# Pairs of PSUM banks for the counts of a graph layer: one copy for two node groups

## The chip, the cores and the metric

The kernel runs on one core of one Trainium2 chip. The metric is the device time of one execution in microseconds, the median over several runs; lower is better. One execution was also profiled, and its trace is what the readings below come from.

## The reference

One layer of a graph network over 12,500 nodes with 128 features and 200,000 edges, of 4 types, sorted by target node:

```python
h = jnp.maximum(_layernorm(x, axis=-1), 0.0)
xs = h[src]
for i in range(4):                        # edge types
    mask = (edge_type_4 == i)[:, None]
    msgs = msgs + jnp.where(mask, xs @ W[i] + b[i], 0.0)
x = x + jax.ops.segment_sum(msgs, dst, num_segments=12500)
```

The targets are drawn as 12500 * u**2, so low node numbers get very many edges and high ones few.

## The kernel before

The kernel works in three stretches: a preparation (up to about 200 us), a long middle (to about 1550 us), and a short end.

**Preparation.** Every row of x is normalized and put as a table `htab` of three 16-bit parts in device memory. The first 568 chunks of 128 edges (the "dense" edges, with low target nodes) are sorted into slots.

**The middle** weaves two kinds of work into one stream of instructions, whose order for TensorE (PE), VectorE (DVE) and ScalarE (ACT) is the order in which the code emits them. SyncE (SP) and GpSimd (POOL) get theirs from a scheduler.

*The dense work* (`dense_work`) takes the dense target nodes in 19 batches of up to 31 units; a unit is a group of up to three nodes or node groups (580 units in all). For each batch:

- `count` makes, for each unit, a matrix of how often each source node (and edge type) occurs. DVE makes two one-hot matrices per slot (`o2`, L1068, and `o1`, L1076), three sets of slots ahead. One matmul per slot (L1101) adds to a count bank of 396 columns; a unit has one or two slots, now and then more. The finished bank is copied to the SBUF tile `counts` by ACT (L1109). The copy is not emitted at once: it goes into the list `owed`, and the function `settle(owed)` emits it when the next unit is finished, or when another user of the same pool asks for a bank.
- `multiply` passes over the table for a batch that is already counted: SP loads three table rows of 128 nodes at a time (`hs`, five buffers), ACT decodes the counts into `dec` (L1169, four buffers, emitted two loads ahead), and PE adds up into the bank `pa` (L1215 with the raw counts, L1207 with `dec`). At the end ACT copies `pa` to `sd` (L1253), and `tail` multiplies it by the weights (L1260); DVE adds the result to `acc` (L1279).

While a batch is counted, the one before it is multiplied. `dense_work` takes whichever of the two is less far along, with the count kept ahead, so that steps of one matmul of the count alternate with steps of six matmuls of the pass.

*The sparse work* takes the other chunks of 128 edges in groups of up to 16. POOL gathers the rows of `htab` (L590), DVE makes one-hots (L608), and in `sum_up` PE multiplies four chunks into one bank `ps` (L643), so that a full group fills four of them, which ACT copies to `sb` (L633). This copy waits in a list of its own, `sums_owed`, until the next `ps` bank is asked for. Between the third and the fourth `ps` bank, `weigh` takes a bank for the group's own counts (four short matmuls, L660), which ACT copies to `cnt` (L664) at once; later it forms `py` (L667, L669), which DVE adds to a ring of sums (L732). From time to time a piece of the ring is transposed (`leave`, L765), added to x by DVE (L770) and stored. Seven times `prep_steps` transposes indices of edges (L375, L376), which ACT copies out.

**The PSUM banks** of a core are eight, and before the change they are given out so: the pool `x_ps` has four single banks, for the count of a unit, for `tail`, `leave`, `prep_steps` and the group counts of `weigh`; `s_ps` has two, for `ps`; `y_ps` and `a_ps` have one each, for `py` and `pa`. A pool gives a new tile any of its banks that is free, and the first writer waits for the last reader of what lay there.

**The end** begins when the dense work is done (`dense_out` is set): the last sparse groups, and the transposes and stores of all dense nodes.

Of the kernel before, what the change touches and what calls it, by code (L numbers as in the profile page):

```python
# [35 lines left out]
F32 = mybir.dt.float32  # L36
# [10 lines left out]
PSUM = bass.MemoryType.PSUM  # L47
# [3 lines left out]
P = 128  # L51
EPS = 1e-5
UN = 3
G = 16
SG = 4
WIN = 32
ROOM = 6
C0 = 568
UB = 31
# [10 lines left out]
OT = 4  # L70
# [17 lines left out]
def kernel(  # L88
# [10 lines left out]
    nc = tc.nc  # L99
    N, D = x.shape  # L100
    E = src.shape[0]
    NT, _, DO = w.shape
# [18 lines left out]
    q = E0 / E  # L121
# [92 lines left out]
    NB = NW * NT  # L214
# [62 lines left out]
    spool = mid.enter_context(tc.tile_pool(name="typed", bufs=2))  # L277
    x_ps = mid.enter_context(tc.tile_pool(name="x_ps", bufs=4, space=PSUM))
    s_ps = mid.enter_context(tc.tile_pool(name="s_ps", bufs=2, space=PSUM))
    y_ps = mid.enter_context(tc.tile_pool(name="y_ps", bufs=1, space=PSUM))  # L280
    a_ps = mid.enter_context(tc.tile_pool(name="a_ps", bufs=1, space=PSUM))
    raw_room = ExitStack()
    aheads = raw_room.enter_context(tc.tile_pool(name="aheads", bufs=4))
# [63 lines left out]
    def prep_steps(m, prep):  # L347
# [267 lines left out]
    def settle(of):  # L615
        while of:
            of.pop(0)()

    adds = []
    finish = []  # L620
# [28 lines left out]
    def weigh(t0, g, oh, sb, last):  # L649
        win = window_of(C0 + t0)  # L650

        def bank(own):
            settle(owed)
            to = y_ps.tile([P, G * WIN], F32, name="py") if own else x_ps.tile([P, G * WIN], F32, name="pt")
            return to[:, : G * win].rearrange("p (g n) -> p g n", g=G)

        ohv = oh.rearrange("p g (t n) -> p g t n", t=NT)
        pc = bank(False)
        for t in range(NT):
            nc.tensor.matmul(  # L660
                pc[t * CG : (t + 1) * CG, :g, :], three, ohv[:, :g, t, :], start=True, stop=True, tile_position=(0, t * CG)
            )
        cnt = spool.tile([P, G * KM // NT], BF16, name="cnt", bufs=1)[:, : G * win].rearrange("p (g n) -> p g n", g=G)
        nc.scalar.copy(cnt[:, :g], pc[:, :g])  # L664
        yield True
        py = bank(not last)
# [89 lines left out]
    def leave(j0, j1, of, c0):  # L756

        nf = min(j1, N // P) - j0
        xt = seen_out.pop(j0) if j0 in seen_out else fetch(j0, j1)
        settle(owed)  # L760
        pt = x_ps.tile([P, OT, DO], F32, name="pt")
        for j in range(j0, j1):
# [12 lines left out]

        return rest

# [69 lines left out]
    def check_all():  # L847
# [4 lines left out]
        nc.vector.tensor_copy(many[:, 2:3], held)  # L852
        pb = x_ps.tile([P, 3], F32, name="pt")
        ones = outp.tile([P, P], F32, name="ones", bufs=1)
# [189 lines left out]
    def count(now, room):  # L1044
# [6 lines left out]
        order = sorted((n / len(of), i) for of in like.values() for n, i in enumerate(of))  # L1051
        for _, i in order:
# [38 lines left out]
        yield 0.0  # L1091
        counts = now[1] = room().tile([P, NW + 1, UB * NT], I32, name="counts")
        for n, of in enumerate(sets):
            supply(n)
            for k, (i, s, by, first, last) in enumerate(of):
# [3 lines left out]
                if first:  # L1099
                    pb = x_ps.tile([P, NB + NT], F32, name="pt")  # L1100
                one = nc.tensor.matmul(pb, o1, o2, start=first, stop=last)  # L1101
# [4 lines left out]
                if last:  # L1106
                    settle(owed)
                    owed.append(
                        lambda i=i, pb=pb: nc.scalar.copy(  # L1109
                            counts[:, :, i * NT : (i + 1) * NT], pb.rearrange("p (b t) -> p b t", t=NT)  # L1110
                        )
                    )
                done += 1
# [37 lines left out]
    def multiply(now):  # L1151
# [104 lines left out]
        def tail(sd):  # L1256
            settle(owed)
            py = x_ps.tile([P, 3 * UB], F32, name="pt")
            for t in range(NT):
# [21 lines left out]

            tails.append(rest)

# [277 lines left out]
    for gi, (t0, g) in list(enumerate(zip(starts, sizes)))[RAW:]:  # L1561
# [56 lines left out]
        if work is None and not dense_out:  # L1618
# [178 lines left out]
```

## Time and profile before

| | |
|---|---|
| median of 3 runs | 1589.8 us (1585.2 to 1591.06) |
| the profiled execution | 1605.82 us, its span 1604.1 us |
| granted TensorE clock, mean | 0.930 |
| PE busy | 1317.4 us (82%) |
| ACT busy | 1077.8 us (67%) |
| DVE busy | 1004.4 us (63%) |
| POOL busy | 966.3 us (60%) |

A group of instructions is named by its line, its engine, its operation and its tiles (written tile <- read tiles). "Idle before" is time in which the engine stood still ahead of such an instruction, with what ended it; "issue" is time in which nothing that the profile shows was waited for. A row of the timeline gives a start in us from the span's start, a duration in us, and merges instructions of one line that follow each other (x6).

### The profile page before, as it was taken

Reading aid. Unit: us, or ns where it says so; the run is one execution under the profiler, and the core shown is the slowest. Engines: PE = TensorE matmul, PEld = TensorE weight load, DVE = VectorE, ACT = ScalarE, POOL = GpSimd, SP = SyncE. Lnnn points to the kernel's source line nnn. Section 1 sums busy time; section 2 is a strip of 40 time slices with the busy share of each in tenths; the row PEclk is TensorE's granted clock in tenths of the full one; section 3 lists DMA queues with packets and bytes.
Section 4 is the critical chain, followed back from the end, with each engine's and each line's share of the span. In section 5 each row is a group of like instructions: output and inputs, shape, how many; then the busy total and the mean of one; then the engine's idle time right before and its main releaser. Section 6 shows DMA issues by size and latency. Waiting matters only on the chain.

```text
span 1604.1 us, 30332 instructions
## 1 busy us (share of the span) xinstructions
PE 1317.4 (82%) x9232; PEld 899.3 (56%) x9232; DVE 1004.4 (63%) x5138; ACT 1077.8 (67%) x1815; POOL 966.3 (60%) x1024
## 2 busy tenths in 40 slices
PE   4876876688889887988889888888888888888885
PEld 1334654466566665656556565665656565565654
DVE  7784466647677765766665575656656565666524
ACT  5675433577677776777677776877777777767651
POOL 6525566666666666666666665666666666666662
PEclk9885798799999999999999999999999999999997
DMA  7542398476676666667676765766666666656762
GB/s 210 186 168 69 113 294 279 123 240 216 192 219 211 216 200 204 209 206 225 190 228 207 227 212 183 229 200 213 216 215 201 207 207 202 215 187 209 254 190 74
DMA packets 184629, 322.55 MB, mean 201 GB/s; under 512 B 30243, under 2 KB 82524, under 8 KB 184460
## 3 DMA queue, kind: packets, MB, share of 16 engines
q1 hardware_dynamic: 132716, 214.63, 42.1%
q0 software_dynamic: 46992, 96.30, 20.0%
q10 hardware_dynamic: 4752, 9.64, 1.6%
q8 instruction: 73, 1.20, 0.3%
q14 instruction: 96, 0.79, 0.1%
HBM read 294.78 MB, written 25.67 MB: 200 GB/s over the span
## 4 chain that ended last, share of the span: by engine, by line
PE 64%; issue 10%; DMA 8%; ACT 7%; DVE 6%; another core or an unknown queue 4%; SPq 1%; DVEq 0%; ACTq 0%
PE pa L1207 16%; PE pa L1215 15%; PE pt L1101 10%; DMA hs<-dtab 7%; PE py L669 6%; PE ps L643 6%; ACT dec L1169 3%; PE pt L1260 2%; PE pa L1237 1%; ACT counts L1109 1%; DVE o L1068 1%; PE ps L701 1%; DVE o L1076 1%; DVE ring L732 1%
## 5 line engine op out<-in xcount | busy, mean ns | idle before, releaser
L590 POOL DMA_INDIRECT hm<-htab,srcT x947 | 915.0, 966 | 570.0 <-issue 207.0
L1169 ACT ACTIVATE dec<-counts 128x1116 fp32r<-128x1116 uint8 (+1 forms) x594 | 662.2, 1136 | 46.4 <-PE pa L1207 12.6
L1068 DVE TENSOR_SCALAR o<-iota_n,hkT 128x392 bf16<-128x392 f16 x1069 | 354.3, 331 | 387.1 <-PE pt L1101 184.6
L1215 PE MATMUL pa<-counts,hs 128*128 128x372 fp8e4 x1764 | 370.9, 336 | 80.6 <-DMA hs<-dtab 37.1
L1207 PE MATMUL pa<-dec,hs 128*128 128x372 f32 x1764 | 411.9, 364 | 29.6 <-ACT dec L1169 14.9
L1109 ACT CAST counts<-pt 128x396 int32<-128x396 f32 x580 | 278.8, 496 | 184.4 <-PE pt L1101 43.7
L1207 PEld LDWEIGHTS pa<-dec,hs 128*128 128x128 f32 x1764 | 309.0, 193 | 68.7 <-issue 30.1
L1101 PE MATMUL pt<-o,o 128*128 128x396 bf16 x1069 | 292.8, 344 | 53.7 <-issue 27.0
L1215 PEld LDWEIGHTS <-hs 128*128 128x128 f16 x1764 | 160.2, 99 | 234.4 <-issue 81.3
L1076 DVE TENSOR_SCALAR o<-iota_b,loT,byT 128x128 bf16<-128x128 bf16 x647 | 213.4, 330 | 0.0
L643 PE MATMUL ps<-oh,hm 128*128 128x72 bf16 (+7 forms) x2841 | 185.0, 201 | 26.6 <-issue 20.6
L643 PEld LDWEIGHTS <-hm 128*128 128x128 f16 x2841 | 149.4, 101 | 101.9 <-issue 54.4
L732 DVE TENSOR_TENSOR ring<-ring,py 128x18 f32 (+6 forms) x912 | 158.6, 174 | 58.4 <-issue 19.3
L608 DVE TENSOR_SCALAR oh<-iota_b,keyT 128x72 bf16<-128x72 bf16 (+7 forms) x947 | 161.8, 257 | 39.3 <-PE pa L1207 23.4
L633 ACT ACTIVATE sb<-ps 128x288 f32<-128x288 f32 (+8 forms) x237 | 99.5, 421 | 108.0 <-PE ps L643 32.2
L1101 PEld LDWEIGHTS <-o 128*128 128x128 bf16 x1069 | 86.6, 99 | 84.6 <-issue 31.2
L669 PE MATMUL py<-sb,wsb 128*128 128x288 f32 (+6 forms) x456 | 123.6, 414 | 0.8 <-issue 0.8
L1076 DVE TENSOR_SCALAR o<-iota_b,loT 128x128 bf16<-128x128 bf16 x422 | 121.7, 288 | 0.0
L669 PEld LDWEIGHTS py<-sb,wsb 128*128 128x128 f32 x456 | 84.1, 195 | 25.0 <-issue 3.9
L664 ACT CAST cnt<-pt 128x288 bf16<-128x288 f32 (+10 forms) x62 | 24.3, 393 | 96.8 <-remote 38.7
L574 POOL DMA_INDIRECT hx<-in_x_dram,srcT x48 | 46.1, 961 | 39.9 <-DVE varr L493 11.0
L1237 PE MATMUL pa<-counts,hs 128*128 128x264 fp8e4 x294 | 45.8, 300 | 11.9 <-DMA hs<-htab 7.1
(251 smaller groups left out, 804.1 us busy)
## 6 DMA issues: line engine op xcount, KB each, us to landing
hs<-dtab SPq DMA_DIRECT2D x576, 288.0 KB
hm<-htab,srcT POOLq DMA_INDIRECT x947
htab<-h SPq DMA_DIRECT2D x32, 288.0 KB
hs<-htab SPq DMA_DIRECT2D x32, 288.0 KB
dtab<-dec ACTq DMA_DIRECT2D x32, 288.0 KB
xo<-in_x_dram SPq DMA_DIRECT2D x23, 256.0 KB
out_dram<-xo SPq DMA_DIRECT2D x23, 256.0 KB
hm<-in_x_dram SPq DMA_DIRECT2D x18, 192.0 KB
```

The costliest lines, as they stand in the source:

```text
L590: one = nc.gpsimd.indirect_dma_start(out=hm[:, (i - h0) * D3 : (i - h0 + 1) * D3], out_offset=None, in_=htab, in_offset=bass.IndirectOffse ...
L608: nc.vector.tensor_scalar(oh[:, i, :], iota_b[:, :K], keyf[:, at : at + 1], None, ALU.is_equal)
L643: nc.tensor.matmul(ps[:, i - i0, :], rows(i, c), oh[:, i, :], start=(c == 0), stop=(c == 2))
L669: nc.tensor.matmul(py[:, :g, :], wsb[:, t, :], sb[0][:, :g, t, :], start=False, stop=(t == NT - 1))
L732: nc.vector.tensor_tensor(to, to, of(i), ALU.add)
L1068: one = nc.vector.tensor_scalar(o2[:, k, :NB], iota_n, hkT[:, s : s + 1], None, ALU.is_equal)
L1076: one = nc.vector.tensor_scalar(o1[:, k], iota_b, loT[:, s : s + 1], by, ALU.is_equal, ALU.mult)
L1101: one = nc.tensor.matmul(pb, o1, o2, start=first, stop=last)
L1109: lambda i=i, pb=pb: nc.scalar.copy(counts[:, :, i * NT : (i + 1) * NT], pb.rearrange("p (b t) -> p b t", t=NT))
L1169: nc.scalar.activation(decoded[n][:, : j1 - j0, :nv].rearrange("p j (m v) -> p j m v", m=3), by_digit[:, j0:j1, : nu * NT * 4].rearrange(" ...
L1207: nc.tensor.matmul(to.rearrange("p (m v) -> p m v", m=3), row.bitcast(F32R)[:, D // 2 :], decoded[j // DS][:, j % DS, :nv].rearrange("p (m ...
L1215: nc.tensor.matmul(to.rearrange("p (m v) -> p m v", m=3), row[:, :D], counts[:, j, : nu * NT * 4].rearrange("p (v m) -> p m v", m=4)[:, :3 ...
```

## The change

Inside the middle, the four single banks of `x_ps` become two pairs of banks (pool `z_ps`, opened when the preparation ends and closed when the dense work is done).

- Two units that follow each other in `count` write the two banks of one pair, and one ACT instruction copies both (`keep_pair`, 2 x 396 elements in a partition instead of 396). The copy goes into `owed` when the second unit is finished. A batch of 31 units has 15 pairs and a last unit alone.
- `tail`, `leave` and `prep_steps` take a whole pair (`pair()`) and use one bank of it.
- The group counts of `weigh` take a bank of `s_ps`, the pool of two that `ps` uses. Asking for it emits the copy that waits in `sums_owed`, and no longer the one in `owed`.
- Asking for a pair emits what waits in `owed`, and also what waits in a new list `unadded`: DVE's additions out of a pair that `tail` or `leave` filled.
- After the dense work, four single banks are opened again (`x2_ps`), and all runs as before.

```diff
+    unadded = []
+
+    def pair():
+        settle(owed)
+        settle(unadded)
+        return z_ps.tile([P, 2, 512], F32, name="pz")
+
+    def bank():
+        if dense_out:
+            return x_ps.tile([P, 512], F32, name="pt")
+        settle(sums_owed)
+        return s_ps.tile([P, 512], F32, name="ps")
...
-        settle(owed)
-        pg = x_ps.tile([P, 2, P], F32, name="pt")
+        pg = (bank() if dense_out else pair()[:, 0, :])[:, : 2 * P].rearrange("p (q e) -> p q e", q=2)
...
     def weigh(t0, g, oh, sb, last):
...
-        def bank(own):
-            settle(owed)
-            to = y_ps.tile([P, G * WIN], F32, name="py") if own else x_ps.tile([P, G * WIN], F32, name="pt")
+        def bank_of(own):
+            to = y_ps.tile([P, G * WIN], F32, name="py") if own else bank()
...
     def leave(j0, j1, of, c0):
...
-        settle(owed)
-        pt = x_ps.tile([P, OT, DO], F32, name="pt")
+        pt = (bank() if dense_out else pair()[:, 0, :]).rearrange("p (j o) -> p j o", o=DO)
...
-        return rest
+        if dense_out:
+            return rest
+        todo = [rest]
+        unadded.append(lambda: settle(todo))
+        return lambda: settle(todo)
...
+        def keep_pair(pz, us):
+            to = counts.rearrange("p b (i t) -> p i b t", t=NT)
+            to = to[:, us[0] : us[-1] + 1 : max(1, us[-1] - us[0])]
+            nc.scalar.copy(to, pz[:, : len(us), : NB + NT].rearrange("p m (b t) -> p m b t", t=NT))
...
                 if first:
-                    pb = x_ps.tile([P, NB + NT], F32, name="pt")
+                    m = place[i]
+                    if m % 2 == 0:
+                        two = [pair(), sorted(order[m : m + 2])]
+                    pb = two[0][:, two[1].index(i), : NB + NT]
...
                 if last:
                     settle(owed)
-                    owed.append(
-                        lambda i=i, pb=pb: nc.scalar.copy(
-                            counts[:, :, i * NT : (i + 1) * NT], pb.rearrange("p (b t) -> p b t", t=NT)
-                        )
-                    )
+                    if m % 2 or m + 1 == len(order):
+                        owed.append(lambda two=two: keep_pair(*two))
...
         def tail(sd):
-            settle(owed)
-            py = x_ps.tile([P, 3 * UB], F32, name="pt")
+            py = pair()[:, 0, : 3 * UB]
...
-            tails.append(rest)
+            unadded.append(rest)
+            tails.append(lambda: settle(unadded))
...
     building.close()
+    ahead_ps.close()
+    z_ps = ahead_ps.enter_context(tc.tile_pool(name="z_ps", bufs=2, space=PSUM))
...
             counting.close()
+            ahead_ps.close()
+            x_ps = ahead_ps.enter_context(tc.tile_pool(name="x2_ps", bufs=4, space=PSUM))
```

How this moves instructions at the place between the third and the fourth `ps` bank of a group is shown by ACT's order there. The group is the same in both pieces; `ps_9603` and `ps_9396` are its third `ps` bank, `pt_9709` and `ps_9499` the bank of its group counts. ACT before:

```order
L1109 CAST counts_9311<-pt_9565 128x99x4 [waits PE_49]
L1109 CAST counts_9311<-pt_9586 128x99x4 [waits PE_49]
L1169 ACTIVATE dec_9629<-counts_8191 128x1116 [waits Activation_49]
L1169 ACTIVATE dec_9694<-counts_8191 128x1116 [waits PE_49,Activation_49]
L1109 CAST counts_9311<-pt_9626 128x99x4
L1109 CAST counts_9311<-pt_9685 128x99x4 [waits PE_49]
L664 CAST cnt_9714<-pt_9709 128x256 [waits PE_49]
L633 ACTIVATE sb_9519<-ps_9603 128x256
```

ACT with the change:

```order
L1192 ACTIVATE dec_9419<-counts_8023 128x1116 [waits Activation_49]
L1114 CAST counts_9113<-pz_9381 128x2x99x4 [waits PE_49]
L1192 ACTIVATE dec_9485<-counts_8023 128x1116 [waits PE_49,Activation_49]
L646 ACTIVATE sb_9314<-ps_9396 128x256 [waits PE_49]
L676 CAST cnt_9504<-ps_9499 128x256 [waits PE_49]
```

The copy of the third `ps` bank now stands ahead of the copy of the group counts, and there are fewer copies of counts around it.

PE at the same place before; `ps_9721` is the group's fourth `ps` bank:

```order
L660 LDWEIGHTS three_218
L660 MATMUL pt_9709<-oh_9071,three_218 32x256
L660 LDWEIGHTS three_218
L660 MATMUL pt_9709<-oh_9071,three_218 32x256
L643 LDWEIGHTS hm_9018 [waits DMASW4_49]
L643 MATMUL ps_9721<-oh_9071,hm_9018 128x64
L643 LDWEIGHTS hm_9018
```

PE with the change, where `ps_9510` is that fourth bank:

```order
L672 LDWEIGHTS three_218
L672 MATMUL ps_9499<-oh_8877,three_218 32x256
L672 LDWEIGHTS three_218
L672 MATMUL ps_9499<-oh_8877,three_218 32x256
L656 LDWEIGHTS hm_8826 [waits DMASW4_49]
L656 MATMUL ps_9510<-oh_8877,hm_8826 128x64 [waits Activation_49]
L656 LDWEIGHTS hm_8826
```

PE's instructions stand in the same order, but the first matmul into the fourth bank now waits for ACT: its bank is that of `ps_9396`.

A second place, on PE, is where a piece of the ring has just been transposed while a unit was being counted. PE before (`pt_16328`, `pt_16383` and `pt_16389` are the banks of three units that follow each other):

```order
L1101 LDWEIGHTS o1_16184
L1101 MATMUL pt_16328<-o2_1715,o1_16184 128x396
L1207 MATMUL pa_15844<-dec_16257,hs_16330 128x372 x3
L1207 MATMUL pa_15844<-dec_16275,hs_16332 128x372 [waits Activation_49]
L1207 MATMUL pa_15844<-dec_16275,hs_16332 128x372 x2
L1101 LDWEIGHTS o1_16184
L1101 MATMUL pt_16383<-o2_1715,o1_16184 128x396 [waits Activation_49]
L1101 LDWEIGHTS o1_16265 [waits DVE_49]
L1101 MATMUL pt_16389<-o2_1715,o1_16265 128x396 [waits Activation_49]
```

PE with the change (the transposes took the pair `pz_15950`; `pz_15933` is the pair of counts that was open meanwhile, `pz_15994` the next one):

```order
L1127 LDWEIGHTS o1_15792
L1127 MATMUL pz_15933<-o2_1719,o1_15792 128x396
L1230 MATMUL pa_15462<-dec_15863,hs_15935 128x372 x3
L1230 MATMUL pa_15462<-dec_15880,hs_15937 128x372 x3
L1127 LDWEIGHTS o1_15792
L1127 MATMUL pz_15933<-o2_1719,o1_15792 128x396
L1127 LDWEIGHTS o1_15871 [waits DVE_49]
L1127 MATMUL pz_15994<-o2_1719,o1_15871 128x396 [waits Activation_49]
```

The last matmul of one pair is followed at once by the first of the next in both. With the change that one waits for ACT's copy of the very pair just finished, since the transposes hold the other pair; before, it waited for a bank that had been filled earlier, one of four.

More of the change, by code (lines that the diff above doesn't have):

```diff
@@ L281 @@
     a_ps = mid.enter_context(tc.tile_pool(name="a_ps", bufs=1, space=PSUM))
+    ahead_ps = mid.enter_context(ExitStack())
+    x_ps = ahead_ps.enter_context(tc.tile_pool(name="x_ps", bufs=4, space=PSUM))
     raw_room = ExitStack()
@@ L650, in weigh @@
         win = window_of(C0 + t0)
-        def bank(own):
-            settle(owed)
-            to = y_ps.tile([P, G * WIN], F32, name="py") if own else x_ps.tile([P, G * WIN], F32, name="pt")
+        def bank_of(own):
+            to = y_ps.tile([P, G * WIN], F32, name="py") if own else bank()
             return to[:, : G * win].rearrange("p (g n) -> p g n", g=G)
         ohv = oh.rearrange("p g (t n) -> p g t n", t=NT)
-        pc = bank(False)
+        pc = bank_of(False)
         for t in range(NT):
@@ L665, in weigh @@
         yield True
-        py = bank(not last)
+        py = bank_of(not last)
         nc.tensor.matmul(py[:, :g, :], b128, cnt[:, :g, :], start=True, stop=False)
@@ L852, in check_all @@
         nc.vector.tensor_copy(many[:, 2:3], held)
-        pb = x_ps.tile([P, 3], F32, name="pt")
+        pb = bank()[:, :3]
         ones = outp.tile([P, P], F32, name="ones", bufs=1)
@@ L1051, in count @@
         order = sorted((n / len(of), i) for of in like.values() for n, i in enumerate(of))
-        for _, i in order:
+        order = [i for _, i in order]
+        place = {i: m for m, i in enumerate(order)}
+        for i in order:
             of = slots_of(vs[i])
```

1 line of the change is left out of this document (removed).

## The prediction

> **What bounds the kernel now.** I read the page's busy times and its chain first, then the middle as one stretch (the columns are PE, PEld, DVE, ACT, POOL, granted clock, DMA share, GB/s), then what PE waits for.
>
> ```profile
> PE 1317.4 (82%) x9232; PEld 899.3 (56%) x9232; DVE 1004.4 (63%) x5138; ACT 1077.8 (67%) x1815; POOL 966.3 (60%) x1024
> PE 64%; issue 10%; DMA 8%; ACT 7%; DVE 6%; another core or an unknown queue 4%; SPq 1%; DVEq 0%; ACTq 0%
> 300.00:1548.00 1248.00, 1079.75 (x7797) 749.25 (x7794) 781.85 (x4034) 912.08 (x1383) 778.59 (x810) 0.97 0.68 211
> PE pa L1215 <- DMA hs<-dtab: 37.1, 39, 2.4
> PE pa L1207 <- ACT dec L1169: 14.9, 20, 2.6
> PE pa L1215 <- ACT sd L1253: 7.7, 4, 3.5
> PE pt L1101 <- ACT counts L1109: 6.4, 4, 4.1
> PE ps L643 <- ACT sb L633: 4.9, 3, 4.3
> PE pt L1260 <- ACT sd L1253: 4.5, 1, 4.5
> ```
>
> PE makes the chain: 64% of the end time lies on it, and in the middle it is busy 1079.75 of 1248 us (87%), ACT 73%. PE is not full, though: it stands still for 168 us there. Little of that is ACT's doing. The five rows in which work of the middle waits for ACT sum to 14.9 + 7.7 + 6.4 + 4.9 + 4.5 = 38.4 us. So a faster ACT can give 38.4 us at the very most, and PE waits for PSUM banks (the rows of `counts` and `sb`) for only 11.3 us. With four single banks and two for `ps`, banks are hardly ever late. That is what the change puts at risk.
>
> **ACT's saving.**
>
> ```profile
> L1109 ACT CAST counts<-pt 128x396 int32<-128x396 f32 x580 | 278.8, 496 | 184.4 <-PE pt L1101 43.7 <-PE ps L643 38.3 <-remote 32.2
> L1536 ACT COPY xo<-pa 128x512 f32<-128x512 f32 x1 | 0.6, 592 | 0.0
> 176.21 2.87 ACT L1109 CAST counts<-pt 128x396 int32<-128x396 f32 x7
> ```
>
> A copy out of PSUM costs 496 ns for 396 elements and 592 for 512, so 96 / 116 = 0.83 ns an element. A pair (792) then costs 496 + 396 x 0.83 = 824 ns, 168 less than two. Eighteen batches of 31 units and one of 22 make 18 x 15 + 11 = 281 pairs: 281 x 0.168 = 47 us less ACT time. But copies that follow each other overlap: seven took 2.87 us, 410 ns each, 86 less than the row's mean. Between busy neighbours a removed instruction so saves 168 - 86 = 82 ns, in all 23 us. I take 23, since ACT is busy for three quarters of the middle. The Trainium skill ("ScalarE: Activation LUTs", section "What ACT_TABLE_LOAD costs") says that back-to-back ACTIVATEs overlap by about 93 ns; by it the saving would be 75 ns a pair, 21 us, an estimate from that page. The row of seven bears it out, and it speaks against the change: merging instructions saves less than their fixed cost.
>
> 23 us is 2.5% of ACT's 912 us. Of the 38.4 us that PE waits for ACT I take 5 away (nothing below, all 38.4 above).
>
> **Two pairs instead of four banks.** I put the trace's times beside the new order of instructions and asked, at each of the 299 places where a pair of counts is used again, how long after its last matmul the next user's first matmul stands. The median is 4.6 us; for the four single banks the same reading gives 6.3. A pair needs two hand-overs and the copy. A hand-over takes 0.05 us:
>
> ```profile
> 783.88 0.47 ACT L1253 ACTIVATE sd<-pa 128x372 f32<-128x372 f32 x1
> 784.40 1.96 PE L1215 MATMUL pa<-counts,hs 128*128 128x372 fp8e4 x6 [1.07 <-ACT sd L1253]
> 788.48 0.31 PE L660 MATMUL pt<-oh,three 128*32 128x288 bf16 x4
> 788.84 0.40 ACT L664 CAST cnt<-pt 128x288 bf16<-128x288 f32 x1 [1.29 <-PE pt L660]
> ```
>
> ACT ends at 784.35 and PE starts at 784.40; PE ends at 788.79 and ACT starts at 788.84. So a pair is back after 0.05 + 0.82 + 0.05 = 0.92 us if ACT is free. At 29 places there is less time than that, at nine of them none: one shown in the orders above, where transposes hold the other pair. It is this one:
>
> ```profile
> 1092.48 1.16 ACT L1169 ACTIVATE dec<-counts 128x1116 fp32r<-128x1116 uint8 x1
> 1092.60 0.51 PE L1101 MATMUL pt<-o,o 128*128 128x396 bf16 x2
> 1092.94 0.66 PE L1215 MATMUL pa<-counts,hs 128*128 128x372 fp8e4 x3
> ```
>
> The first matmul of the row of two ends one pair (at about 1092.93), the second (from 1092.78) opens the next in the same banks. If ACT were free, PE would stand until 1092.93 + 0.92 = 1093.85, 1.1 us. But ACT decodes until 1093.64, and the copy comes behind that: 1093.64 + 0.82 + 0.05 = 1094.51, 1.7 us. Done so for all 299 places, the sum is 14 us at 29 places with ACT free, and 113 us at 99 places with ACT as late as in the trace (the end of the instruction ahead of the copy in ACT's new order). The first of the 99 is late by 0.2 us at the end of the preparation, the last by 0.8 us near the end of the middle:
>
> ```profile
> 175.48 1.17 PE L1101 MATMUL pt<-o,o 128*128 128x396 bf16 x3
> 176.21 2.87 ACT L1109 CAST counts<-pt 128x396 int32<-128x396 f32 x7
> ...
> 1478.05 1.14 ACT L1169 ACTIVATE dec<-counts 128x1116 fp32r<-128x1116 uint8 x1
> 1479.09 0.50 PE L1101 MATMUL pt<-o,o 128*128 128x396 bf16 x2
> ```
>
> I take 45, between 14 and 113, nearer the lower end: ACT's lateness in the trace holds copies that go, and an ACT for which PE has waited is no longer behind at the next place.
>
> **Group counts in `s_ps`.** Here `ps` loses its slack: the fourth `ps` bank of a group now reuses the third, with only the group counts between. Before, a median of 9 us lay between the uses of a bank. In 38 groups the two stand within 3.5 us of each other, and the evict of the third (0.42 us, L633) must fit in.
>
> ```profile
> L633 ACT ACTIVATE sb<-ps 128x288 f32<-128x288 f32 (+8 forms) x237 | 99.5, 421 | 108.0 <-PE ps L643 32.2
> 313.60 0.32 PE L643 MATMUL ps<-oh,hm 128*128 128x48 bf16 x6
> 315.37 1.14 ACT L1169 ACTIVATE dec<-counts 128x1116 fp32r<-128x1116 uint8 x1
> ...
> 660.04 2.16 ACT L1169 ACTIVATE dec<-counts 128x1116 fp32r<-128x1116 uint8 x2
> 661.25 0.35 PE L643 MATMUL ps<-oh,hm 128*128 128x64 bf16 x6
> ...
> 1352.92 1.16 ACT L1169 ACTIVATE dec<-counts 128x1116 fp32r<-128x1116 uint8 x1
> 1355.49 0.41 PE L643 MATMUL ps<-oh,hm 128*128 128x88 bf16 x6
> ...
> 1524.33 0.43 PE L643 MATMUL ps<-oh,hm 128*128 128x96 bf16 x6
> 1525.47 1.14 ACT L1169 ACTIVATE dec<-counts 128x1116 fp32r<-128x1116 uint8 x1 [1.77 <-PE ps L643]
> ```
>
> These are four of the 38, the first and the last among them: PE's first matmul into the fourth bank, and the work that stands ahead of the evict in ACT's new order. In the group of the orders above that is a pair of decodes which ends at 662.20; with 0.42 for the evict and 0.05 the bank is free at 662.67, 1.4 us after PE wants it at 661.25. Near 1355 the evict is in time: the decode ahead of it ends at 1354.08. Over the 38 groups the sum is 77 us, at 32 of them; with an ACT that is never behind it is nothing. I take 35, for the reason just given.
>
> **What stands behind these waits, and what hides them.** PE takes its queue in order, so behind a wait for a bank stand the matmuls of the pass, of the next counts and of the sparse group; DVE's one-hots (L1068) and POOL's gathers (L590), which wait for PE's progress, come later with it. Some of it is paid back: while PE stands, loads of `hs` and decodes under way go on, and PE finds less of its 37.1 + 14.9 = 52 us of waits for them. I take 35 of these 52 off (bounds 0 and 52).
>
> **Edits at nothing.** `tail`, `leave` and the index transposes take a pair each; that is in the 299 places, since they stand in the rotation. Their DVE additions now come at the next request for a pair, so that a late load of x would hold DVE and the one-hots behind it. Such a wait shows once before (5.2 us, for L770), and DVE is at 63% in the middle: 0, with 20 as an upper end. Opening the pairs waits for the last bank of the preparation, once, about 1 us; PE is idle around it.
>
> **Sum.** -5 + 45 + 35 - 35 = +40 us. The profiled execution has a span of 1604.1 us, which becomes 1644; its own time of 1605.8 becomes 1645.8. It stands 16 us above the median of 1589.8, so the forecast for the median is 1589.8 + 40 = 1630 us.
>
> **The rivals.**
>
> *ACT is in time (faster).* With fewer copies in its queue ACT may no longer be behind when a bank is wanted. Then the pairs cost their 14 us, the `ps` banks nothing, and the 38.4 us of waits for ACT mostly go: 14 - 30 = -16, 1574 us. For it: ACT idles 184.4 us before L1109 and 108.0 before L633, so it is not short of time. Against it: that idle time is waiting for PE, in order, after which ACT runs behind in a burst of copies and decodes, as at 313.60. It decides if ACT's lag at the fourth `ps` bank falls from some 2 us (77 / 38) below about 0.9 us, the least distance of 1.35 us less evict and hand-over. Chance 0.22.
>
> *All cancels (same).* The bank waits are only taken out of PE's other waits: within 8 us of 1590. Within 0.5%, or 8 us, a measurement of this kernel cannot be told from no change. Chance 0.10.
>
> *Full price (much slower).* ACT stays as late as in the trace and nothing is hidden: 113 + 77 - 5 = +185 at the most, with 35 hidden +150, 1740 us. Against it: it takes the lateness of before for granted in a kernel where PE keeps stopping for ACT. Chance 0.13; from 1670 to 1740, with some 0.04 of it under 1695.
>
> *DVE is held by loads of x.* Up to 20 us on top, 1650. One row for it. Chance 0.05.
>
> **The numbers.** The forecast has 0.50, with a range of its own of 1600 to 1670 (the bank waits at half of the 80 that I took, 40 - 5 - 25, and at one and a half times, 120 - 5 - 35). Slower by over 0.5%: 0.50 + 0.13 + 0.05 = 0.68; within: 0.10; faster: 0.22. The range that should hold 8 in 10 runs from 1572 (half of the faster case, 0.11) over the same, the forecast and DVE (0.65) to 1695 (0.04 of the full price).
>
> **What would show it.** Right: PE's waits for the copy of pairs and for `sb` at L656 (the new line of the `ps` matmuls) rise from 11.3 us together to some 60 to 90; ACT's copies are about 299 at 0.82 us, its busy time down by 20 to 50 us; PE's waits for `hs` fall. Wrong: those waits stay under 20 us, or a pair's copy takes clearly more than 0.82 us, or DVE turns up as what PE waits for.

## The result, and the profile after

The changed kernel takes 1611.74 us (median; 1607.01 to 1619.29) where the kernel before takes 1589.8 on the same chip: a ratio of 1.0144 with a 95% interval of 1.0109 to 1.0179, so 22 us slower. The profiled execution took 1619.29 us with a span of 1617.5 us, 13.4 us over the span of before. (The two differences differ because the profiled execution of before stood 16 us above its median, and this one 7.6.)

The page's busy times and its chain by engine, and the same middle stretch as one window (PE, PEld, DVE, ACT, POOL, granted clock, DMA share, GB/s):

```profile
PE 1306.4 (81%) x9232; PEld 918.5 (57%) x9232; DVE 1006.0 (62%) x5138; ACT 1060.3 (66%) x1534; POOL 969.4 (60%) x1024
PE 63%; ACT 13%; issue 8%; DMA 6%; DVE 5%; another core or an unknown queue 4%; POOL 2%; SPq 0%; DVEq 0%; ACTq 0%; POOLq 0%
300.00:1548.00 1248.00, 1055.22 (x7676) 753.67 (x7674) 774.18 (x3990) 884.26 (x1122) 766.42 (x796) 0.96 0.68 208
```

ACT has less to do (1060.3 us against 1077.8), yet its share of the chain has risen from 7% to 13%. In the same 1248 us of the middle PE does 24.5 us less. PE's waits say for what it stands. `pz` is the new name of the pairs; L1127 are the matmuls of the counts, L1282 those of `tail`, L656 those of `ps`, L1238 and L1230 those of the pass:

```profile
PE ps L656 <- ACT sb L646: 53.8, 22, 5.4
PE pz L1127 <- ACT counts L1114: 48.8, 37, 6.5
PE pa L1238 <- DMA hs<-dtab: 19.1, 16, 3.3
PE pz L1127 <- issue: 15.3, 21, 2.2
PE pz L1282 <- ACT counts L1114: 13.1, 7, 5.1
PE pa L1238 <- issue: 7.3, 13, 1.0
PE pa L1230 <- ACT dec L1192: 6.6, 12, 1.0
PE pa L1230 <- issue: 3.3, 5, 1.0
```

Two smaller rows belong beside them:

```profile
PE ps L656 <- DMA hm<-htab,srcT: 11.7, 6, 2.7
PE ps L656 <- ACT dec L1192: 8.6, 6, 3.0
```

The waits for banks were 6.4 + 4.9 = 11.3 us; now the three largest are 53.8 + 48.8 + 13.1 = 115.7 us. But the time in which PE is not busy rose only from 1604.1 - 1317.4 = 286.7 to 1617.5 - 1306.4 = 311.1, by 24.4 us. (The span rose by only 13.4 us because PE's busy time fell by 11.0 us with the same instructions; why it fell is open, and the ends of matmuls are modelled.) So on balance some 80 of the 104 us of new waits were taken out of others. `hs` fell from 37.1 to 19.1. The row of `dec` at L1230 fell from 14.9 to 6.6, but the wait only moved: with L656 and L1238, all rows that end in `dec` came to 19.0 us, against 16.7 before. Waits for `hm` even rose, from 0.9 to 11.7. The largest part came from rows that end in "issue", which before were

```profile
PE pa L1215 <- issue: 32.7, 48, 2.5
PE pt L1101 <- issue: 27.0, 33, 6.3
PE pa L1207 <- issue: 14.3, 29, 1.2
```

so 74.0 us, of which 25.9 are left (all rows that end in "issue": 130.1 and 73.5). Waits for DVE's one-hots fell from 12.8 to 1.8 us and those for `sd` from 12.2 to 2.6. What such idle time consists of the profile does not say; it gives way when PE stands elsewhere.

ACT's groups (line, busy time, mean ns, idle time before), and the copies of counts by themselves (min, median and max in ns, first and last start in us):

```profile
L1114 ACT CAST counts<-pz 128x792 int32<-128x792 f32 (+1 forms) x299 | 238.1, 799 | 155.0 <-PE pz L1127 54.7 <-remote 22.1 <-PE ps L656 20.4
L646 ACT ACTIVATE sb<-ps 128x288 f32<-128x288 f32 (+8 forms) x237 | 97.6, 412 | 186.3 <-PE py L681 80.1 <-remote 37.6 <-PE ps L656 17.9
```

```profile
L1114 ACT CAST counts<-pz x299: 477/818/865, 132.4 to 1506.3; 128x792 int32<-128x792 f32 x132, 128x396 int32<-128x396 f32 x18
```

The copies are 299 as forecast, with a mean of 799 ns. The eighteen single copies are in that mean; the median, nearly always a pair, is 818 ns (forecast 824). By the fixed cost and the rate that the Trainium skill gives for an ACTIVATE with immediate scale and bias ("ScalarE: Activation LUTs", section "What ACT_TABLE_LOAD costs") a pair would take 186 + 792 x 0.833 = 846 ns, an estimate from that page; the trace agrees within 28 ns.

When the loss comes is read from `sd`, which ACT writes once a batch, after and then before, in the same view:

```profile
L1276 ACT ACTIVATE sd<-pa x19: 392/478/483, 281.9 to 1570.4; 128x372 f32<-128x372 f32 x18, 128x264 f32<-128x264 f32 x1
```

```profile
L1253 ACT ACTIVATE sd<-pa x19: 392/480/494, 295.0 to 1555.0; 128x372 f32<-128x372 f32 x18, 128x264 f32<-128x264 f32 x1
```

The first batch ends 13.1 us earlier than before, the last 15.4 us later. So the change gains up to the first batch and loses 28.5 us in the 18 batches that follow.

### The profile page after: what moved, and what is told of

It is laid out like the page before. It is cut to its first block, busy times and chain, and to the rows that moved or that the text cites. A ratio compares the mean times of both kernels' runs of the same rounds, so it can differ in the third digit from the quotient of the medians.

```text
span 1617.5 us, 30046 instructions
## 1 busy us (share of the span) xinstructions
PE 1306.4 (81%) x9232; PEld 918.5 (57%) x9232; DVE 1006.0 (62%) x5138; ACT 1060.3 (66%) x1534; POOL 969.4 (60%) x1024
## 4 chain that ended last, share of the span: by engine, by line
PE 63%; ACT 13%; issue 8%; DMA 6%; DVE 5%; another core or an unknown queue 4%; POOL 2%; SPq 0%; DVEq 0%; ACTq 0%; POOLq 0%
PE pa L1230 17%; PE pa L1238 14%; PE pz L1127 10%; PE py L681 6%; PE ps L656 6%; ACT dec L1192 6%; ACT counts L1114 4%; DMA hs<-dtab 2%; DMA hm<-htab,srcT 2%; POOL hm L590 2%; PE pz L1282 1%; PE pa L1260 1%; DMA hs<-htab 1%; ACT sb L646 1%
## 5 line engine op out<-in xcount | busy, mean ns | idle before, releaser
L1192 ACT ACTIVATE dec<-counts 128x1116 fp32r<-128x1116 uint8 (+1 forms) x594 | 652.1, 1129 | 49.1 <-PE pa L1230 17.7
L1230 PE MATMUL pa<-dec,hs 128*128 128x372 f32 x1764 | 416.6, 370 | 10.6 <-ACT dec L1192 6.6
L1238 PE MATMUL pa<-counts,hs 128*128 128x372 fp8e4 x1764 | 360.0, 336 | 33.4 <-DMA hs<-dtab 19.1
L1127 PE MATMUL pz<-o,o 128*128 128x396 bf16 x1069 | 299.5, 349 | 73.3 <-ACT counts L1114 48.8
L1230 PEld LDWEIGHTS pa<-dec,hs 128*128 128x128 f32 x1764 | 319.4, 199 | 45.9 <-issue 17.3
L1114 ACT CAST counts<-pz 128x792 int32<-128x792 f32 (+1 forms) x299 | 238.1, 799 | 155.0 <-PE pz L1127 54.7
L1238 PEld LDWEIGHTS <-hs 128*128 128x128 f16 x1764 | 166.0, 99 | 196.4 <-issue 69.7
L656 PE MATMUL ps<-oh,hm 128*128 128x72 bf16 (+7 forms) x2841 | 181.7, 202 | 97.9 <-ACT sb L646 53.8
L656 PEld LDWEIGHTS <-hm 128*128 128x128 f16 x2841 | 153.0, 101 | 166.6 <-issue 118.2
L1127 PEld LDWEIGHTS <-o 128*128 128x128 bf16 x1069 | 87.4, 101 | 76.2 <-issue 39.6
L676 ACT CAST cnt<-ps 128x288 bf16<-128x288 f32 (+7 forms) x58 | 23.0, 396 | 71.9 <-PE pz L1127 33.0
```

The source lines that it names most:

```text
L656: nc.tensor.matmul(ps[:, i - i0, :], rows(i, c), oh[:, i, :], start=(c == 0), stop=(c == 2))
L1114: nc.scalar.copy(to, pz[:, : len(us), : NB + NT].rearrange("p m (b t) -> p m b t", t=NT))
L1192: nc.scalar.activation(decoded[n][:, : j1 - j0, :nv].rearrange("p j (m v) -> p j m v", m=3), by_digit[:, j0:j1, : nu * NT * 4].rearrange(" ...
L1230: nc.tensor.matmul(to.rearrange("p (m v) -> p m v", m=3), row.bitcast(F32R)[:, D // 2 :], decoded[j // DS][:, j % DS, :nv].rearrange("p (m ...
L1238: nc.tensor.matmul(to.rearrange("p (m v) -> p m v", m=3), row[:, :D], counts[:, j, : nu * NT * 4].rearrange("p (v m) -> p m v", m=4)[:, :3 ...
```

## The experiments

They ran on three chips, on which the kernel before took 1605.57 us (`a_share` to `c_two`), 1346.12 us (`after_again` to `e_copy`) and 1348.19 us (`f_again` to `b_soon`). Times are therefore compared as ratios to the kernel before on the same chip, and directly only within one of these sets. (A ratio differs by up to 0.2% from the quotient of the two medians given here.) The kernel before has a trace from the first chip alone. My theory: the loss is banks that ACT gives back late. Its rival: the pairs alone, or the group counts in `s_ps` alone, make the loss. A second question came up on the way: whether it matters where a copy stands in ACT's queue. ACT takes this queue in order: in the trace of before, the eight instructions shown above as ACT's order ran in just that order, from 657.42 to 666.65 us.

**One half alone (`a_share`).** The kernel before, with only the group counts moved to `s_ps`.

```diff
-            settle(owed)
-            to = y_ps.tile(...) if own else x_ps.tile([P, G * WIN], F32, name="pt")
+            if own: ...
+            else:
+                settle(sums_owed)
+                to = s_ps.tile([P, 512], F32, name="ps")
```

> The kernel before with one part of the change alone: the group counts of the sparse work lie in the pool of the two ps banks; the four single banks stay for the counts of units. Theory 'banks' (PE's waits for banks make the loss, and both parts have a share of it): about half of the loss, some +10 us over before (1600 us); PE waits for the evicts of ps (sb) for 40 to 55 us, and for copies of counts for under 10 us. Rival 'pairs only' (the pairs make all of the loss, the ps waits are paid back by other waits): within 4 us of before.

Measured: 1608.21 us, ratio 1.0025 (1.0005 to 1.0046). PE's waits:

```profile
PE ps L643 <- ACT sb L633: 63.1, 26, 5.0
PE pa L1222 <- DMA hs<-dtab: 17.3, 19, 2.9
```

The wait for `sb` is as large as in the changed kernel and larger than the 35 us that I took, but it costs only 2.6 us of time (4.0 by the ratio). "Banks" had expected some 10 us, "pairs only" 4 at most. In a kernel with four count banks, PE gets the wait back nearly whole.

**The other half alone (`b_single`, `b_pairs`).** Both leave out the group counts: the four matmuls of `weigh`, their copy to `cnt` and the matmul with the bias (the bias is missing from the sums). `b_single` is otherwise the kernel before, `b_pairs` the changed one, so that between them stand the pairs alone.

```diff
-        pc = bank(False)
-        for t in range(NT):
-            nc.tensor.matmul(pc[t * CG : (t + 1) * CG, :g, :], three, ohv[:, :g, t, :], ...)
-        nc.scalar.copy(cnt[:, :g], pc[:, :g])
...
-        nc.tensor.matmul(py[:, :g, :], b128, cnt[:, :g, :], start=True, stop=False)
```

> The kernel before without the group counts of the sparse work: their four matmuls, their copy and the matmul with the bias are left out of every group, so the output lacks the bias of those edges. It is the base for the next run. Both theories: some 10 to 25 us under before (1565 to 1580), with PE's waits for copies of counts under 10 us.

> The changed kernel without the group counts (the same part left out), so that the pairs of banks act alone and nothing shares the ps banks. Theory 'banks': +8 to +14 us over the run with single banks and no group counts; PE waits for copies of counts for 45 to 65 us, for sb under 10 us. Rival 'ps only' (the shared ps banks make all of the loss): within 4 us of that run, or below it by what ACT saves.

Measured: 1601.36 us, ratio 0.9963 (0.9943 to 0.9983), and 1629.69 us, ratio 1.015 (1.0128 to 1.0173). The pairs alone cost 28.3 us, where "banks" had expected 8 to 14. `b_single` is only 4.2 us under before, where 10 to 25 were expected. PE's waits, of `b_single` first:

```profile
PE pa L1206 <- DMA hs<-dtab: 85.8, 68, 3.3
PE pt L1092 <- ACT counts L1100: 7.3, 9, 2.1
```

```profile
PE pa L1229 <- DMA hs<-dtab: 54.3, 55, 3.8
PE pz L1118 <- ACT counts L1105: 53.1, 40, 5.5
PE pz L1273 <- ACT counts L1105: 15.6, 5, 8.2
PE pz L767 <- ACT counts L1105: 11.3, 6, 3.3
```

On this chip the loss is the pairs', not the shared `s_ps`. Two of the rows are not counts waiting for counts: L1273 is `tail` and L767 is `leave`, 26.9 us in 11 waits. They are few, and each is long: 8.2 us at most.

`b_single` also shows how much slack PE has with four single banks. Its PE has 24.0 us less to do than that of `a_share` (1292.5 us busy against 1316.5) and hardly waits for `sb` (5.6 us at L643), yet its time is only 6.9 us shorter: PE waits 85.8 us for `hs` instead of 17.3. That fits a wait for `sb` standing largely in place of one for `hs`, though no run changes that alone. Why the waits for pairs are not paid in the same way is open.

**Is it the merged instruction (`c_two`)?** The changed kernel, with each bank of a pair copied by an instruction of its own, both at the pair's place.

```diff
-            nc.scalar.copy(to, pz[:, : len(us), : NB + NT].rearrange(...))
+            for k, i in enumerate(us):
+                nc.scalar.copy(counts[:, :, i * NT : (i + 1) * NT], pz[:, k, : NB + NT].rearrange(...))
```

> The changed kernel with each pair copied by two instructions of one bank each, so that ACT's saving is taken back and the banks stay as they are. Theory 'banks': ACT is busy for 20 to 45 us more, the pair comes back 0.1 us later, and the time is 2 to 10 us above the changed kernel (1614 to 1622). Rival 'long copy' (an instruction of 0.82 us that waits for two units holds up the decodes behind it): as fast as the changed kernel or faster, 1600 to 1612.

Measured: 1635.91 us, ratio 1.0205 (1.0183 to 1.0227), more than the 1.0144 of the change. ACT's copies and PE's wait for them:

```profile
L1113 ACT CAST counts<-pz 128x396 int32<-128x396 f32 x580 | 256.3, 498 | 150.9 <-PE pz L1128 51.0 <-remote 25.3 <-PE pa L1231 18.1
PE pz L1128 <- ACT counts L1113: 52.7, 37, 6.0
```

The wait for the pairs is about that of the changed kernel (52.7 us beside 48.8), with 18 us more of copies on ACT. So it is not the long instruction that makes it. ACT's copies grew by less than the 20 to 45 us expected. What merging gains is less sure. Against the ratio of the change it is 0.6%, some 10 us, but over two chips. Put together from its parts on this chip (1629.69 of `b_pairs`, 1605.57 - 1601.36 = 4.2 for the group counts, 2.6 for sharing), the changed kernel, which did not run on this chip, would come to 1636.5, no less than `c_two`. So the gain lies between nothing and 10 us, if the parts add up, which no run shows.

**The other users of the pairs (`after_again`, `f_others`).** Besides the counts, 45 others take a whole pair for one bank: 19 `tail`s, 19 `leave`s and 7 `prep_steps`. `f_others` gives them a bank of `s_ps`, so that the pairs serve counts only; `after_again` is the changed kernel on that chip.

```diff
-        pg = (bank() if dense_out else pair()[:, 0, :])[:, : 2 * P].rearrange(...)
+        pg = bank()[:, : 2 * P].rearrange(...)
...
-        pt = (bank() if dense_out else pair()[:, 0, :]).rearrange("p (j o) -> p j o", o=DO)
+        pt = bank().rearrange("p (j o) -> p j o", o=DO)
...
-            py = pair()[:, 0, : 3 * UB]
+            py = bank()[:, : 3 * UB]
```

(Each request of an `s_ps` bank then also emits the additions in `unadded`.)

> The changed kernel once more, on the chip of the next three runs, as their base. All theories: 1.1 to 1.8% above before, as measured.

> The changed kernel with the 45 other users (the tails, the transposes of the ring and those of the edge indices) taken out of the pairs and put into the two ps banks, so that the pairs serve the counts alone. Theory 'other users' (a whole pair lent out leaves one pair for the counts, and these places make most of the loss: in the trace of the changed kernel 57 of 93 us of PE's waits ahead of pair users stand next to one): 10 to 20 us under the changed kernel, within 6 us of before; PE's waits for copies of counts fall from 62 us to 25 to 40. Rival 'two slots' (two pairs are too few even for the counts alone): within 6 us of the changed kernel.

Measured: 1372.99 us, ratio 1.0221 (1.0195 to 1.0247), and 1357.44 us, ratio 1.0074 (1.0054 to 1.0095). `after_again` is outside the 1.1 to 1.8% expected of it; on this chip the change costs more. PE's waits, of `after_again` and then of `f_others`:

```profile
PE pz L1127 <- ACT counts L1114: 18.8, 25, 1.4
PE ps L656 <- ACT sb L646: 18.3, 27, 2.9
```

```profile
PE ps L658 <- ACT sb L647: 17.6, 31, 1.2
PE pz L1129 <- ACT counts L1116: 6.6, 9, 1.6
```

15.5 of the 26.9 us that the change costs on this chip go when these 45 requests leave the pairs (by the ratios two thirds). All PE's waits for copies of counts, those of `tail` and `leave` included, fall from 23.3 to 6.6 us. The 11.3 us that are left are more than the 6 expected. While one of the 45 holds a pair, the counts have one pair left, and each unit pair must wait for the copy of the one before. One thing more differs: at these 45 places the request no longer emits the waiting copy of counts, so that some copies come later too. No run separates the two.

**The copy's place in ACT's queue (`g_early`, `e_copy`).** In the changed kernel a pair's copy is emitted when the next pair is asked for, with a step of the pass in between. `e_copy` emits it right where the second unit ends. `g_early` has two copies: the first unit's where the second unit ends, the second's when the next pair is asked for.

```diff
                 if last:
                     settle(owed)
                     if m % 2 or m + 1 == len(order):
-                        owed.append(lambda two=two: keep_pair(*two))
+                        keep_pair(*two)
```

```diff
-                    if m % 2 or m + 1 == len(order):
-                        owed.append(lambda two=two: keep_pair(*two))
+                    owed.append(
+                        lambda i=i, pb=pb: nc.scalar.copy(counts[:, :, i * NT : (i + 1) * NT], pb.rearrange(...))
+                    )
```

> The changed kernel with each bank of a pair copied by an instruction of its own as soon as its own unit is finished (in the list of owed copies, as before the change); the pair is still given back as a whole. Theory 'waits for the second unit' (the first bank lies full until the second is, and its copy comes in one late burst): 8 to 16 us under the run with two copies at the pair's end, that is at the changed kernel's time or 5 us under it. Rival 'slots alone' (only the number of slots counts): at the time of two copies at the pair's end, 4 to 10 us above the changed kernel.

> The changed kernel with the pair's copy put into ACT's queue right when the second unit is finished, and not at the next step of the count, so that it stands ahead of decodes that come between. Theory 'banks': 3 to 10 us under the changed kernel, PE's waits for copies of counts down by a quarter or more. Rival 'decodes held up' (a copy that ACT has to wait for holds the decodes behind it): the same as the changed kernel or up to 8 us slower, with PE's waits for decodes up.

Measured: `g_early` 1400.72 us, ratio 1.0415 (1.0394 to 1.0436); `e_copy` 1392.82 us, ratio 1.036 (1.0341 to 1.0379), 19.8 us over `after_again`. Of the two theories for `g_early` neither saw so much, and of those for `e_copy` neither: "banks" had the sign wrong, and "decodes held up" had at most 8 us, with longer waits for decodes, of which PE shows none. In `g_early` ACT stands before the copies, and PE waits for both kinds of banks, longer than in `after_again`:

```profile
ACT counts L1135 <- PE pz L1127: 92.8, 119, 5.5
PE ps L656 <- ACT sb L646: 29.1, 36, 3.5
PE pz L1127 <- ACT counts L1135: 23.9, 32, 1.7
```

ACT's group of copies, of `after_again` and then of `e_copy`, and PE's waits in `e_copy`:

```profile
L1114 ACT CAST counts<-pz 128x792 int32<-128x792 f32 (+1 forms) x299 | 240.1, 805 | 59.6 <-PE pz L1127 46.9 <-issue 4.4 <-DVE dec L1207 3.7
```

```profile
L1114 ACT CAST counts<-pz 128x792 int32<-128x792 f32 (+1 forms) x299 | 238.4, 800 | 119.4 <-PE pz L1127 101.8 <-issue 12.0 <-DVE ring L744 2.5
```

```profile
PE ps L656 <- ACT sb L646: 33.9, 40, 3.7
PE pa L1238 <- ACT sd L1276: 13.8, 16, 1.3
PE pz L1127 <- ACT counts L1114: 12.0, 17, 0.9
```

The pairs do come back earlier: PE waits 12.0 us for them, not 18.8. But ACT reaches the copy before PE has filled the pair, stands there for 101.8 us instead of 46.9, and what is queued behind it comes late: the wait for `sb` grows from 18.3 to 33.9 us, that for `sd` from 5.4 to 13.8.

This accounts for half of the loss at most. Between the two profiled executions, 21.6 us apart, `e_copy` is 10.7 us late already at the first `sd` (253.1 us against 242.4), and `g_early` 10.9 us. Up to there PE waits for `sb` at L656 about as long in both (5.2 and 4.9 us), while ACT stands 32.2 us before the copies instead of 14.1. How that becomes time in the first batch is open. The waits for `sb` and `sd` grow in the 18 batches behind it, where `e_copy` loses 11.4 us.

**The copy later, the evict earlier (`f_again`, `f_late`, `f_late_d`), and the copy earlier in the kernel before (`b_soon`).** `f_again` is `f_others` once more. `f_late` takes one line out of it, so that a pair's copy is emitted a unit later. `f_late_d` also emits the evict (the copy to `sb`) of a full group's third `ps` bank at once. `b_soon` is the kernel before, with each unit's copy emitted where the unit ends.

```diff
     def pair():
-        settle(owed)
         settle(unadded)
```

```diff
-            sums_owed.append(lambda i0=i0, i1=i1, ps=ps: evict(i0, i1, ps))
+            if i0 == 2 * SG and g == G:
+                evict(i0, i1, ps)
+            else:
+                sums_owed.append(lambda i0=i0, i1=i1, ps=ps: evict(i0, i1, ps))
```

```diff
                 if last:
-                    settle(owed)
-                    owed.append(lambda i=i, pb=pb: nc.scalar.copy(...))
+                    nc.scalar.copy(counts[:, :, i * NT : (i + 1) * NT], pb.rearrange("p (b t) -> p b t", t=NT))
```

> Pairs for counts alone, tails and transposes in s_ps, run again beside the two kernels that are built on it. 'Banks' (the 45 other users of the pairs cost about two thirds of the loss): 1.007 to 1.010 of the kernel before, that is 10 to 16 us above it if before is near 1600 us, 9 to 13 us above it if before is near 1350 us. If 1.007 was the luck of one chip: 1.012 or more.

> As f_again, but the request of a pair no longer emits the copy that is owed; the pair's copy is emitted when the first unit of the next pair ends, a whole unit after its own pair is full, as each copy of the kernel before was. 'Place of the copy' (in ScalarE's in-order queue a copy that stands too early holds up what is behind it): ScalarE's idle time ahead of the copies falls by 10 us or more against f_again, the time falls by 5 to 15 us against it, to between 0.997 and 1.003 of the kernel before. 'Banks': with two pairs and the copy a unit later, a pair comes free one unit later, TensorE's waits for the copies of counts rise by 15 us or more and the time rises by 5 to 15 us against f_again.

> As f_late, and the copy out of the third bank of a dense group's sums is emitted as soon as that bank is full, not at the next request of an s_ps bank. 'Sums are given back late': TensorE's waits for sb fall by a third or more against f_late, and the time falls by 2 to 8 us. 'Place of the copy': the evict now stands earlier in ScalarE's queue and ScalarE waits in front of it; the time rises by 3 to 15 us against f_late.

> The kernel before with one edit: each unit's counts are copied as soon as the unit is counted, not when the next unit is or a bank is asked for. No pair, no other bank, no other user. 'Place of the copy': ScalarE's idle time ahead of the copies rises by 20 us or more and the time rises by 10 to 25 us, about as much as the whole change cost. 'Banks': copies that come earlier give four banks back earlier, nothing else changes; the time stays within 4 us of the kernel before.

Measured:

| kernel | median, us | ratio to before | 95% interval |
|---|---|---|---|
| `f_again` | 1356.22 | 1.0063 | 1.0039 to 1.0086 |
| `f_late` | 1354.22 | 1.0038 | 1.0018 to 1.0059 |
| `f_late_d` | 1342.74 | 0.9962 | 0.9944 to 0.9981 |
| `b_soon` | 1350.81 | 1.0019 | 0.9998 to 1.004 |

PE's waits for the pairs and for `ps`, of `f_again`, `f_late` and `f_late_d`, then PE's for `ps` in `b_soon` and ACT's for the counts there:

```profile
PE ps L658 <- ACT sb L647: 20.0, 28, 4.6
PE pz L1129 <- ACT counts L1116: 7.1, 10, 1.6
```

```profile
PE ps L657 <- ACT sb L646: 14.2, 29, 1.2
PE pz L1128 <- ACT counts L1115: 12.0, 15, 1.6
```

```profile
PE pz L1131 <- ACT counts L1118: 14.2, 15, 2.0
PE ps L657 <- ACT sb L646: 2.7, 7, 0.6
```

```profile
PE ps L643 <- ACT sb L633: 1.6, 3, 1.0
```

```profile
ACT counts L1107 <- PE pt L1101: 50.2, 64, 5.7
```

`f_again` repeats `f_others` (1.0063 beside 1.0074). `f_late` is 2 us below it and their intervals overlap, so the unit's delay is not shown to gain anything: the wait for `sb` falls by 5.8 us, that for the pairs rises by 4.9. "Place of the copy" had asked for 5 to 15 us, "banks" for a loss of as much, and neither came. ACT did stand 19.9 us less before the copies (49.0 us in `f_again`, 29.1 in `f_late`), so that this standing has no fixed price in time.

`f_late_d` settles the `ps` banks: the wait for `sb` all but goes (14.2 to 2.7 us), and 11.5 us of time go with it, more than the 2 to 8 expected. Here, with the pairs in place and the 45 other users in the two `ps` banks, the waits for `sb` do cost time, unlike in `a_share`, and a copy placed earlier pays. This version beats the changed kernel and also the kernel before, by 0.4%. The same early evict in the kernel before was not tried, so how much of the 0.4% needs the pairs is open. The traces point to the first batch. From the first `sd` to the last, `f_late_d` takes 1051.2 us and `b_soon`, with four single banks and early copies, 1051.9; but `f_late_d` has its first `sd` at 245.9 us and `b_soon` at 249.8.

`b_soon` is what my second theory falls on in its plain form. The same early place costs at most 0.4% with four single banks, where `e_copy` lost 1.4% with two pairs. ACT waits for PE in `b_soon` too (50.2 us), but 28.2 of them lie before the first `sd`. Behind it ACT stands 22.0 us before the copies, in `e_copy` 69.6, and PE waits only 1.6 us for `sb` in all. So the early place brings ACT less standing here, and what stands behind it is in less of a hurry. That an early copy is dear only where few banks are left for what stands behind it fits both, but is argued: `e_copy` with `ps` alone in its banks was not tried.

## Why the prediction came out as it did

The direction and the mechanism were right: PE comes to wait for banks that ACT gives back late. The forecast was +40 us, the result +22, inside the forecast's own range of 1600 to 1670. That it came so near is in part luck: two errors cancelled, and of the two halves of the sum nearly all of the loss came from one, the pairs. The two rows named as the sign of being right, of pairs and of `sb` at L656, came to 102.6 us, above the 60 to 90 given. The terms, one by one:

- **ACT's saving, 23 us of ACT time and 5 us of the end.** The copy was right (824 ns forecast, 818 measured). ACT's busy time fell by 17.5 us, a little less than forecast and just outside the 20 to 50 named as a sign. By `c_two` its worth is between nothing and 10 us, which the 5 is in the middle of.
- **Pairs, 45 us of waits.** 48.8 + 13.1 = 61.9 us in the two rows of the changed kernel. The 45 are a quarter below that; taking a value near the lower of the two bounds (14 and 113) was too hopeful. The order of instructions had named a cause, transposes that hold the other pair; `f_others` bears it out, up to the later copies that it brings as well.
- **Group counts in `s_ps`, 35 us of waits.** 53.8 us. The price of the waits was wrong by more than their size: alone, 63.1 us of them cost 2.6 us. The sum took a microsecond of this wait to cost what one of the pairs' costs, and that was wrong.
- **Paid back, 35 us.** This is the step that failed. I allowed only the 52 us of `hs` and `dec` as cover, and 35 of those. About 80 us came back on balance: 18.0 from `hs`, nothing from `dec` in all, 48.1 from the three "issue" rows, which I had not counted as cover, though they were 74 us, and 20.6 from waits for one-hots and `sd`, less new waits such as that for `hm`. The two errors, waits too small (80 forecast, 104 measured) and payback too small (35, 80), partly cancelled: 104 - 80 = 24 of PE's idle time against the forecast 80 - 35 - 5 = 40. The sum also took PE's busy time as fixed; between the profiled executions it fell by 11.0 us.
- **The preparation and the first batch, nothing.** 13.1 us are gained there. On the chip of `a_share` the kernels with pairs were 6 to 10 us early (`b_pairs` 282.6 and `c_two` 282.8 at the first `sd`, `b_single` 288.8, `a_share` 292.8); `c_two` gains without merged copies, so it isn't ACT's saving. Nor do pairs alone make it: `e_copy` and `g_early`, with pairs but earlier copies, come 11 us later than `after_again`. Its cause is open.

Of the rivals, *all cancels* holds for half of the change: sharing `s_ps` cost 0.25%. *ACT is in time* did not come about, but `f_late_d` comes near to it: with the third bank given back at once and the pairs left to the counts, the waits for pairs are 14.2 us and those for `sb` 2.7, about the 14 and the nothing of that rival. The time falls below that of before, by 5 us rather than 16. *Full price* is refuted by the 80 us that came back. Of *DVE held by loads of x* there is no sign: DVE's wait for such a load was 5.2 us before and is 3.8 now, and its one-hots wait for PE.

```profile
DVE o L1085 <- PE pz L1127: 215.4, 96, 14.5
```

What stays open: why a microsecond of waiting for `ps` costs next to nothing beside four single banks (`a_share`) and its full length beside two pairs (`f_late_d`, though on another chip, where PE has less slack).

## What to carry to other kernels

A larger tile out of the same banks makes every other user of the pool take a larger tile as well: count the rare users too, since each leaves the main stream with one buffer for a while, and more than half of this loss went when 45 of them were moved. Before a wait is priced, list all of PE's idle time that can give way to it, also the part the profile can't name: of 104 us of new waits 80 cost nothing here. For an engine that ran its queue in order here, the place of a copy is a choice of its own: an evict for whose bank the next matmul waited gained 11.5 us when it was put earlier. Putting a copy where the engine then stood waiting for it, with such evicts behind it, lost 19.8; half of that fell in the first batch and is not explained, and with four single banks the same edit cost at most 0.4%.

## What the hardware showed unexpectedly

Chips differ far more than the kernels do: the kernel before took 1589.8, 1605.57, 1346.12 and 1348.19 us in the four sets. The changed kernel's times on the first chip and in `after_again` differ by 17%, the granted clock by 5% (0.924 and 0.968). On the faster chip PE stood still for 1365.5 - 1230.2 = 135.3 us, on the first for 311.1. No wait of PE ends in "issue" there, and DMA moved 245 GB/s in the middle where it moved 208 on the first chip. This is `after_again`'s window of 1000 us from 300 on:

```profile
300.00:1300.00 1000.00, 946.20 (x7256) 689.98 (x7255) 739.64 (x3848) 829.19 (x1063) 737.14 (x757) 1.00 0.79 245
```

So new waits had less idle time to be paid from there, which fits the dearer change (2.2% against 1.4%); why the chips differ was not tried.
